# Where the look-ahead work of a chunked recurrent attention stands: one pair of heads ahead in two blocks, or up to two pairs ahead in pieces

## The chip, the cores and the metric

The kernel runs on one core of one Trainium2 chip. The metric is device time in microseconds, the median of repeated runs, and one further execution was recorded by the hardware profiler. Engines are named as in the profile: PE is TensorE's matmul, PEld its weight load, DVE is VectorE, ACT is ScalarE, POOL is GpSimd and SP is SyncE, which issues nearly all transfers here.

## What is computed

Two layers on x of shape 2 x 1024 x 512. Each layer adds to x the product of an attention part and a gated MLP of the layer-normalised input. The change touches the first layer's attention alone, a gated delta rule with 16 heads of 128:

```python
q = silu(causal_dwconv(x @ Wq, qcw, qcb))          # k and v in the same way
alpha = sigmoid(x @ Wa + ba); beta = sigmoid(x @ Wb + bb)
def step(S, inps):
    qt, kt, vt, at, bt = inps
    Sk = einsum('bhvk,bhk->bhv', S, kt)
    err = Sk - vt
    S = at * S - bt * (err[..., None] * kt[:, :, None, :])
    ot = einsum('bhvk,bhk->bhv', S, qt)
    return (S, ot)
o = layernorm(o) * ln_w + ln_b
return (o * sigmoid(x @ Wg)) @ Wo
```

Written step by step, this is 1024 dependent steps. The kernel computes it in chunks of 128 tokens. Inside a chunk the dependence is a lower triangular system, whose matrix L is built from k and the decays; the state S passes from one chunk to the next.

## The kernel before

Heads go in 8 pairs (index `hg`, 0 to 7). A pair holds two heads of two batches, so four sequences side by side, and has 8 chunks (`c`). Projections are made for two chunks at a time (`p`, 0 to 3).

For one pair the work has these parts. `project` (L448) makes q, k or v: matmuls at L455 into the two PSUM buffers `pa`, two evictions by ACT (L467, L471), three taps of the convolution on the DVE (L475), and SiLU on ACT (L483). The gate is projected in the pair's loop at L741. `ahead` (L486) makes for two chunks k, the decays e and the matrices L of 32 x 32 blocks (pkk at L506, lt at L508), and stores all three in DRAM. `invert` (L515) loads the diagonal blocks of all 8 chunks of a pair, 128 blocks on 128 partitions, and inverts them by 31 steps of a multiply into `tl` (L531) and a subtraction from `ml` (L538), each needing the one before, all on the DVE; then it stores them. Counting its set-up and its store, it hands out 33 steps. `within` (L548) loads e and the inverted blocks and makes what a chunk needs without the state. `across` (L586) is the chain of the recurrence: pks from the state (L599), rt on the DVE (L600), transposed into pr (L606), then four block steps of pw (L622), w4 by ACT (L624), pz (L616) and rr by the DVE (L621), then wt, the new state (L638, L644), the output po and its normalisation. `finish` (L678) transposes, gates and stores the previous chunk's output.

The stages in time are these. In the front the input is normalised and transposed and the first layer's MLP runs (48 steps in all, handed out by `some(n)`), with `ahead` and `invert` of pair 0 written between its steps. The front has one PSUM buffer each for `pa` and `pi`. The pairs follow. In pair `hg`, behind each of the chunks 0 to 3 stands a whole `ahead` of the next pair, one for each `p`; behind chunks 4 to 7 stand nine steps each of the next pair's inverse. So k, e, L and the inverse are all one pair ahead. After the last pair come the output projection, which is joined with the MLP's result, and then the second layer.

The order on each engine is not the written one. A scheduler places instructions at build time by modelled readiness, and the written order is the priority among those that are ready. On the chip each engine then works through its own list in that fixed order, with semaphores for the data. A list entry whose data are late holds up all that is behind it on its engine.

Of the kernel before, what the change touches and what calls it, by code (L numbers as in the profile page):

```python
# [19 lines left out]
DRAM = bass.MemoryType.DRAM  # L20
# [7 lines left out]
HG = H // 2  # L28
# [3 lines left out]
IC = INTER // P  # L32
# [20 lines left out]
def cols(ap, n):  # L53

    if len(ap.shape) == 2:
        ap = ap.unsqueeze(2)
    return ap.to_broadcast([ap.shape[0], ap.shape[1], n])


def rep(ap, n):  # L60

    return ap.unsqueeze(1).to_broadcast([ap.shape[0], n, ap.shape[1]])
# [150 lines left out]
def first_layer(ctx, tc, a, cst, minus_half, keep, xnT, od, gd, then):  # L213
# [23 lines left out]

    nc = tc.nc  # L240
    cp = keep

    early = ctx.enter_context(ExitStack())
    pa = early.enter_context(tc.tile_pool(name="at_a", bufs=2))
    kp = early.enter_context(tc.tile_pool(name="at_k", bufs=1))
    dr = ctx.enter_context(tc.tile_pool(name="at_d", bufs=2, space=DRAM))

    pools = {}

# [129 lines left out]
    def some(n):  # L379
        for _ in zip(range(n), beside):  # L380
            pass

    def load_weights(hg, names):
        w = {}
        for n in names:
            pool = kp if n == "wk" else pools["w"]
            w[n] = pool.tile([P, KC, 2 * P], F32, tag=n, name=f"{n}_{hg}")
            nc.sync.dma_start(
                w[n], a[n][:, hg * 256 : (hg + 1) * 256].rearrange("(kc p) n -> p kc n", p=P)
            )  # L390
        return w
# [56 lines left out]
    def project(j, n, hg, p, w, dst):  # L448

        u = f"{n}_{hg}_{p}"  # L450
        for hl in range(2):
            h = hg * 2 + hl
            pp = pools["a"].tile([P, B, 2 * P], F32, tag="pa", name=f"p{u}_{hl}")
            for kc in range(KC):
                nc.tensor.matmul(  # L455
                    pp,
                    lhsT=w[:, kc, hl * P : (hl + 1) * P],
                    rhs=xnT[:, kc, :, p * 2 * P : (p + 1) * 2 * P],
                    start=(kc == 0),
                    stop=(kc == KC - 1),  # L460
                )
            pre = pools["p"].tile([P, B, 2 * P + 4], F32, tag="pre", name=f"pre{u}_{hl}", bufs=3)
            if p == 0:
                nc.gpsimd.memset(pre[:, :, 0:3], 0.0)
            else:
                nc.gpsimd.tensor_copy(pre[:, :, 0:3], halo[:, j, hl, :, 0:3])
            nc.scalar.copy(pre[:, :, 3 : 2 * P + 3], pp)  # L467
            if p < NC // 2 - 1:
                nc.gpsimd.tensor_copy(halo[:, j, hl, :, 0:3], pre[:, :, 2 * P : 2 * P + 3])
            acc = dst[:, 2 * hl : 2 * hl + 2, :]  # L470
            nc.scalar.activation(  # L471
                acc, pp, AF.Identity, scale=cw[:, j, h, 3:4], bias=cb[:, j, h : h + 1]
            )
            for tap in range(3):
                nc.vector.scalar_tensor_tensor(  # L475
                    acc,
                    in0=pre[:, :, tap : tap + 2 * P],
                    scalar=cw[:, j, h, tap : tap + 1],
                    in1=acc,
                    op0=ALU.mult,  # L480
                    op1=ALU.add,
                )
        nc.scalar.activation(dst, dst, AF.Silu)  # L483


    def ahead(hg, p, w, store):  # L486
        u = f"{hg}_{p}"
        ka = pa.tile([P, NS, 2 * P], F32, tag="ka", name=f"ka_{u}")
        project(1, "wk", hg, p, w["wk"], ka)
        nc.sync.dma_start(store["k"][p], ka)  # L490
        for c in (2 * p, 2 * p + 1):
            col = c * H * B + hg * NS
            k = ka[:, :, (c % 2) * P : (c % 2 + 1) * P]

            e = pa.tile([P, NS, P + 4], F32, tag="e", name=f"e_{hg}_{c}", bufs=3)
            nc.gpsimd.memset(e[:, :, 0:1], 0.0)
            g_rows(hg, c, e[:, :, 1 : P + 1])
            nc.vector.tensor_tensor(e[:, :, 1 : P + 1], e[:, :, 1 : P + 1], rep(mask, NS), ALU.add)
            for s in range(NS):
                nc.scalar.activation(  # L500
                    e[:, s, 1 : P + 1], e[:, s, 1 : P + 1], AF.Exp, bias=bcol[:, col + s : col + s + 1]
                )
            nc.sync.dma_start(store["e"][c], e[:, :, 1 : P + 1])
            pkk = pools["i"].tile([P, NS, P], F32, tag="pi", name=f"pkk_{hg}_{c}")
            for s in range(NS):
                nc.tensor.matmul(pkk[:, s, :], lhsT=k[:, s, :], rhs=k[:, s, :], start=True, stop=True)  # L506
            lt = pa.tile([P, NS, P], F32, tag="lt", name=f"lt_{hg}_{c}")
            nc.vector.tensor_tensor(lt, pkk, e[:, :, 0:P], ALU.mult)  # L508
            for bl in range(4):
                nc.sync.dma_start(  # L510
                    store["l"][c, :, :, SLOT[bl] : SLOT[bl] + 4 - bl, :].rearrange("s i b t -> i s (b t)"),
                    lt[32 * bl : 32 * bl + 32, :, 32 * bl :],
                )

    def invert(hg, store):  # L515

# [172 lines left out]
    def new_store(hg):  # L689
        return {  # L690
            "k": dr.tile([NC // 2, P, NS, 2 * P], F32, tag="dk", name=f"dk_{hg}"),
            "e": dr.tile([NC, P, NS, P], F32, tag="de", name=f"de_{hg}"),
            "l": dr.tile([NC, NS, 32, 10, 32], F32, tag="dl", name=f"dl_{hg}"),
        }

    NP = NC // 2
    wk = load_weights(0, ("wk",))
    store = new_store(0)
    for p in range(NP):
        some(IC // 2)  # L700
        ahead(0, p, wk, store)
    for _ in invert(0, store):
        some(1)
    some(NTT * IC)
    front.close()
    for n, bufs in (("w", 2), ("g", 1), ("b", 2)):
# [9 lines left out]
    with tc.issue_after(last["act"].ins):  # L716
        late = None
        for hg in range(HG):
            w = load_weights(hg, ("wq", "wv", "wg"))
            state = None  # L720
            more = hg + 1 < HG
            if more:
                wk = load_weights(hg + 1, ("wk",))
                after = new_store(hg + 1)
                steps = invert(hg + 1, after)
            else:
                early.close()
                joining = then()
            for p in range(NP):
                u = f"{hg}_{p}"  # L730
                kb = pools["b"].tile([P, NS, 2 * P], F32, tag="kb", name=f"kb_{u}")
                nc.sync.dma_start(kb, store["k"][p])
                q = pools["b"].tile([P, NS, 2 * P], F32, tag="q", name=f"q_{u}")
                project(0, "wq", hg, p, w["wq"], q)
                v = pools["b"].tile([P, NS, 2 * P], F32, tag="v", name=f"v_{u}")
                project(2, "wv", hg, p, w["wv"], v)
                gate = pools["b"].tile([P, NS, 2 * P], F32, tag="gate", name=f"gate_{u}")
                for hl in range(2):
                    pg = pools["a"].tile([P, B, 2 * P], F32, tag="pa", name=f"pgate_{u}_{hl}")
                    for kc in range(KC):  # L740
                        nc.tensor.matmul(  # L741
                            pg,
                            lhsT=w["wg"][:, kc, hl * P : (hl + 1) * P],
                            rhs=xnT[:, kc, :, p * 2 * P : (p + 1) * 2 * P],
                            start=(kc == 0),
                            stop=(kc == KC - 1),
                        )
                    nc.scalar.activation(gate[:, 2 * hl : 2 * hl + 2, :], pg, AF.Sigmoid)
                for c in (2 * p, 2 * p + 1):
                    half = slice((c % 2) * P, (c % 2 + 1) * P)  # L750
                    parts = within(hg, c, q[:, :, half], kb[:, :, half], v[:, :, half], store)
                    state, on = across(hg, c, state, parts)
                    if late is not None:
                        finish(*late)
                        if not more and c in (1, 2):
                            joining.load_o()
                    late = (hg, c, gate[:, :, half], on)
                    if more:
                        if c < NP:
                            ahead(hg + 1, c, wk, after)  # L760
                        else:
                            for _ in zip(range(9), steps):
                                pass
            if more:
                for _ in steps:
                    pass
                store = after
        finish(*late)
    return joining

# [369 lines left out]
```

## Time and profile before

| | us |
|---|---|
| median of 3 runs (3357.73 to 3361.75) | 3358.22 |
| the profiled execution's own time | 3359.76 |
| its span | 3357.7 |
| front: start to the first projection of pair 0 | 0 to 324 |
| pairs 0 to 7: to the normalisation of the last chunk | 324 to 1860 |
| pair 1 (last chunk of pair 0 to last chunk of pair 1) | 195.1 |
| pair 6 | 189.5 |
| pair 7 | 150.4 |
| granted TensorE clock, mean | 0.998 |

The page of a profile begins with each engine's busy time as a share of the span, and then cuts the span into 40 slices of about 84 us, with the busy share of each in tenths. In this kernel the slices 5 to 22 are the pairs of heads. A row of the view of windows gives, for one stretch, its start and end, its length, and the busy time and count of each engine. A row of the view of waits gives who waited, for what, the sum, the number of times and the longest. In the timeline each row is a run of like instructions with its start, its duration and, in brackets, the idle time before it.

### The profile page before, as it was taken

How to read it: one execution, taken by the hardware profiler on the slowest of the kernel's cores; microseconds unless marked ns; L12 is line 12 of the kernel's file. 1: busy time of each engine (PE TensorE's matmuls, PEld its weight loads, DVE VectorE, ACT ScalarE, POOL GpSimd, SP SyncE). 2: the span in 40 equal slices, each digit the busy share in tenths (PEclk: the TensorE clock that was granted, in tenths of full speed). 3: DMA queues.
4: the chain of work that ended last, by engine and by line, in shares of the span. 5: the costliest groups of instructions: out<-in, count | busy, mean ns of one | idle time of the engine just before them, and what ended most of it. 6: DMA issues, size and time to landing. Idle time of an engine off the chain costs nothing.

```text
span 3357.7 us, 35998 instructions
## 1 busy us (share of the span) xinstructions
PE 3253.2 (97%) x11734; PEld 1803.9 (54%) x11734; DVE 2079.6 (62%) x4397; ACT 1425.9 (42%) x2480; POOL 865.9 (26%) x1520
## 2 busy tenths in 40 slices
PE   8999999999999999999999999999999999999998
PEld 6677565656565665656566444444444444444443
DVE  4445676676867677686855623666666655555545
ACT  3453676767677677767666000222222200110002
POOL 2000334343343435344344200111121100000102
PEclk9999999999999999999999999999999999999999
DMA  5122443434434343433351653111111100000003
GB/s 168 56 73 77 119 122 102 109 86 126 109 87 127 101 108 87 125 105 95 91 141 43 194 153 101 35 32 32 31 32 32 44 25 19 19 23 22 19 0 125
DMA packets 428699, 268.21 MB, mean 80 GB/s; under 512 B 193888, under 2 KB 368480, under 8 KB 428512
## 3 DMA queue, kind: packets, MB, share of 16 engines
q1 hardware_dynamic: 418208, 248.87, 26.2%
q0 software_dynamic: 5696, 8.65, 0.9%
q10 hardware_dynamic: 4608, 8.39, 0.7%
q8 instruction: 94, 1.54, 0.2%
q14 instruction: 93, 0.76, 0.1%
HBM read 179.71 MB, written 86.11 MB: 79 GB/s over the span
## 4 chain that ended last, share of the span: by engine, by line
PE 43%; DVE 6%; ACT 2%; issue 2%; POOL 2%; DMA 0%; POOLq 0%; DVEq 0%; ACTq 0%
PE po L1005 10%; PE jpo L183 6%; PE pgc L928 3%; PE pgd L928 3%; PE puc L928 3%; PE pua L928 3%; PE pga L928 3%; PE pud L928 3%; PE pgb L928 1%; PE pub L928 1%; DVE ga L886 1%; PE pgate L741 1%; PE pwk L455 1%; PE pwv L455 1%; PE pr L871 1%
## 5 line engine op out<-in xcount | busy, mean ns | idle before, releaser
L1005 PE MATMUL po<-w_d,u 128*128 128x512 f32 x1024 | 456.8, 599 | 10.9 <-DVE acc L1016 5.4
L1005 PEld LDWEIGHTS po<-w_d,u 128*128 128x128 f32 x1024 | 190.0, 190 | 272.0 <-issue 207.3
L948 ACT COPY g<-pga 128x512 f32<-128x512 f32 x32 | 18.7, 586 | 640.1 <-PE pga L928 640.1
L629 POOL COPY wt<-w 32x128 f32<-32x128 f32 x512 | 233.2, 456 | 113.4 <-ACT w L624 91.8
L455 PE MATMUL pwq<-xnT,wq 128*128 128x512 f32 x512 | 251.3, 593 | 0.0
L455 PE MATMUL pwv<-xnT,wv 128*128 128x512 f32 x512 | 240.3, 599 | 9.1 <-ACT q L471 8.4
L455 PE MATMUL pwk<-xnT,wk 128*128 128x512 f32 x512 | 247.0, 594 | 0.0
L1016 DVE TENSOR_TENSOR acc<-acc,po 128x512 f32<-128x512 f32 x240 | 163.0, 682 | 135.6 <-PE po L1005 134.5
L741 PE MATMUL pgate<-xnT,wg 128*128 128x512 f32 x512 | 238.8, 593 | 0.1
L183 PE MATMUL jpo<-wo,jo 128*128 128x512 f32 x512 | 225.0, 592 | 0.0
L475 DVE SCALAR_TENSOR_TENSOR ka<-prewk,cw,ka 128x512 f32<-128x512 f32 x192 | 151.2, 788 | 65.4 <-ACT ka L471 54.8
L475 DVE SCALAR_TENSOR_TENSOR q<-prewq,cw,q 128x512 f32<-128x512 f32 x192 | 149.8, 780 | 55.9 <-ACT q L471 53.8
L475 DVE SCALAR_TENSOR_TENSOR v<-prewv,cw,v 128x512 f32<-128x512 f32 x192 | 155.7, 827 | 42.8 <-ACT v L471 40.6
L622 PEld LDWEIGHTS pw<-rr,ground 128*128 128x128 f32 x512 | 88.8, 188 | 169.8 <-DVE rr L621 121.3
L974 ACT ACTIVATE g<-g 128x512 f32<-128x512 f32 x96 | 60.4, 630 | 261.1 <-DVE g L938 260.9
L616 PEld LDWEIGHTS pz<-w,ground 128*128 128x128 f32 x768 | 119.7, 190 | 84.3 <-ACT w L624 51.2
L183 PEld LDWEIGHTS jpo<-wo,jo 128*128 128x128 f32 x512 | 95.0, 191 | 107.1 <-issue 107.1
L616 PE MATMUL pz<-w,ground 128*128 128x128 f32 x768 | 140.7, 283 | 8.0 <-ACT w L624 8.0
L455 PEld LDWEIGHTS pwv<-xnT,wv 128*128 128x128 f32 x512 | 91.3, 191 | 104.9 <-issue 83.4
L832 POOL TENSOR_TENSOR w_g<-w_g 128x256 f32<-128x256 f32 x16 | 11.9, 741 | 503.8 <-DVE w_g L818 503.8
L673 ACT ACTIVATE on<-po,nm,rs 128x128 f32<-128x128 f32 x256 | 96.3, 457 | 107.0 <-DVE nm L668 107.0
L622 PE MATMUL pw<-rr,ground 128*128 128x128 f32 x512 | 107.4, 292 | 31.2 <-DVE rr L621 27.9
(246 smaller groups left out, 6806.6 us busy)
## 6 DMA issues: line engine op xcount, KB each, us to landing
e<-gr SPq DMA_DIRECT2D x64, 256.0 KB, 4.4
de<-e SPq DMA_DIRECT2D x64, 256.0 KB, 2.6
dk<-ka SPq DMA_DIRECT2D x32, 512.0 KB, 2.8
kb<-dk SPq DMA_DIRECT2D x32, 512.0 KB, 4.7
eb<-de SPq DMA_DIRECT2D x64, 256.0 KB, 2.8
eg<-gr SPq DMA_DIRECT2D x64, 256.0 KB, 3.8
od<-ot SPq DMA_DIRECT2D x64, 256.0 KB, 2.1
jo<-od SPq DMA_DIRECT2D x16, 1024.0 KB, 6.4
```

The lines of the kernel that those rows point to most:

```text
L183: nc.tensor.matmul(po, lhsT=ot[:, h, :], rhs=self.wo[h], start=(h == 0), stop=(h == H - 1))
L455: nc.tensor.matmul(pp, lhsT=w[:, kc, hl * P : (hl + 1) * P], rhs=xnT[:, kc, :, p * 2 * P : (p + 1) * 2 * P], start=(kc == 0), stop=(kc == ...
L475: nc.vector.scalar_tensor_tensor(acc, in0=pre[:, :, tap : tap + 2 * P], scalar=cw[:, j, h, tap : tap + 1], in1=acc, op0=ALU.mult, op1=ALU.add,
L616: nc.tensor.matmul(pz[:, bl, :], lhsT=G[:, SLOT[bb] + bl - bb, :], rhs=w4[:, bb, :], start=(bb == 0), stop=(bb == bl - 1),)
L622: nc.tensor.matmul(pw[:, bl, :], lhsT=G[:, SLOT[bl], :], rhs=rr[:, bl, :], start=True, stop=True)
L629: nc.gpsimd.tensor_copy(dst, w4[r, bl])
L673: nc.scalar.activation(on[:, s, :], po[:, s, :], AF.Identity, scale=rs[:, s : s + 1], bias=nm[:, s : s + 1])
L741: nc.tensor.matmul(pg, lhsT=w["wg"][:, kc, hl * P : (hl + 1) * P], rhs=xnT[:, kc, :, p * 2 * P : (p + 1) * 2 * P], start=(kc == 0), stop=( ...
L928: nc.tensor.matmul(banks[key], lhsT=w[:, i, par, :], rhs=q[:, j, par, :], start=(first and par == 0), stop=(par == 1), skip_group_check=no ...
L974: nc.scalar.activation(ge[key], x, AF.Gelu_apprx_tanh)
L1005: nc.tensor.matmul(po, lhsT=inter[par, h][:, i * P : (i + 1) * P], rhs=wd[:, par, :], start=(par == 0), stop=(par == 1),)
L1016: nc.vector.tensor_tensor(dst, dst, po, ALU.add)
```

## The change

It does four things.

- Where the work made ahead stands. k, e and L are now made two pairs ahead, and the inverse one pair ahead. Pair `hg` therefore has beside it `ahead` of pair `hg + 2` and `invert` of pair `hg + 1`. `ahead` of pairs 0 and 1 and the inverse of pair 0 are in the front; the inverse of pair 1 stands in pair 0. Pair 6 has only an inverse beside it, pair 7 nothing.
- How it is cut. `project` hands over after each of its two heads, and `ahead` after each chunk, so one `ahead` has four pieces and a pair's four have 16. Behind every chunk stand four steps of the inverse (five behind chunk 0) and two pieces.
- The priority of `across` is raised by 40 places.
- The DRAM pool has three buffers rather than two, since three pairs' k, e and L are alive at once. In the front, three MLP steps rather than five stand ahead of each `ahead` of pair 0, and each `ahead` of pair 1 stands behind one step in six of the inverse of pair 0.

```diff
+def done(steps):
+    for _ in steps:
+        pass
...
-    dr = ctx.enter_context(tc.tile_pool(name="at_d", bufs=2, space=DRAM))
+    dr = ctx.enter_context(tc.tile_pool(name="at_d", bufs=3, space=DRAM))
...
                     op0=ALU.mult,
                     op1=ALU.add,
                 )
+            yield
         nc.scalar.activation(dst, dst, AF.Silu)
...
-        project(1, "wk", hg, p, w["wk"], ka)
+        yield from project(1, "wk", hg, p, w["wk"], ka)
...
                     lt[32 * bl : 32 * bl + 32, :, 32 * bl :],
                 )
+            yield
...
+    stores = [new_store(0), new_store(1)]
     wk = load_weights(0, ("wk",))
-    store = new_store(0)
     for p in range(NP):
-        some(IC // 2)
-        ahead(0, p, wk, store)
-    for _ in invert(0, store):
+        some(3)
+        done(ahead(0, p, wk, stores[0]))
+    wk = load_weights(1, ("wk",))
+    for i, _ in enumerate(invert(0, stores[0])):
         some(1)
+        if i % 6 == 1 and i // 6 < NP:
+            done(ahead(1, i // 6, wk, stores[1]))
     some(NTT * IC)
...
             w = load_weights(hg, ("wq", "wv", "wg"))
             state = None
+            store = stores[hg]
             more = hg + 1 < HG
             if more:
-                wk = load_weights(hg + 1, ("wk",))
-                after = new_store(hg + 1)
-                steps = invert(hg + 1, after)
+                steps = invert(hg + 1, stores[hg + 1])
             else:
                 early.close()
                 joining = then()
+            if hg + 2 < HG:
+                wk = load_weights(hg + 2, ("wk",))
+                stores.append(new_store(hg + 2))
+                aheads = itertools.chain.from_iterable(
+                    ahead(hg + 2, p, wk, stores[hg + 2]) for p in range(NP)
+                )
...
-                project(0, "wq", hg, p, w["wq"], q)
+                done(project(0, "wq", hg, p, w["wq"], q))
...
-                    state, on = across(hg, c, state, parts)
+                    with tc.high_priority(40):
+                        state, on = across(hg, c, state, parts)
...
                     if more:
-                        if c < NP:
-                            ahead(hg + 1, c, wk, after)
-                        else:
-                            for _ in zip(range(9), steps):
-                                pass
-            if more:
-                for _ in steps:
-                    pass
-                store = after
+                        done(itertools.islice(steps, 4 if c else 5))
+                    if hg + 2 < HG:
+                        done(itertools.islice(aheads, 2))
```

More of the change, by code (lines that the diff above doesn't have):

```diff
@@ L733, in first_layer @@
                 q = pools["b"].tile([P, NS, 2 * P], F32, tag="q", name=f"q_{u}")
-                project(0, "wq", hg, p, w["wq"], q)
+                done(project(0, "wq", hg, p, w["wq"], q))
                 v = pools["b"].tile([P, NS, 2 * P], F32, tag="v", name=f"v_{u}")
-                project(2, "wv", hg, p, w["wv"], v)
+                done(project(2, "wv", hg, p, w["wv"], v))
                 gate = pools["b"].tile([P, NS, 2 * P], F32, tag="gate", name=f"gate_{u}")
```

## The prediction, made before the changed kernel was run

> **What bounds the kernel now.** I read the page first: busy shares, then the slices.
>
> ```profile
> PE 3253.2 (97%) x11734; PEld 1803.9 (54%) x11734; DVE 2079.6 (62%) x4397; ACT 1425.9 (42%) x2480; POOL 865.9 (26%) x1520
> ...
> PE   8999999999999999999999999999999999999998
> ...
> DVE  4445676676867677686855623666666655555545
> ```
>
> TensorE is in use almost throughout, so the kernel is a stream of matmuls, and what a reordering can win is the time in which that stream stands still. The busy share hides part of it, because the recorded ends of matmuls overlap. I therefore take the pitch from the timeline: six 128x512 matmuls of pwq took 2.74 us with a last one of 0.59, so (2.74 - 0.59) / 5 = 0.43 us each; eight 128x128 ones took 1.06 with a last one of 0.28, so 0.111 us each. What a stretch lasts beyond count times pitch is lost. Next I read stretches bounded by the 4th and 8th chunk of a pair of heads (where nm is written): pair 1 in two halves, then the first half of the last pair, which has nothing made ahead beside it.
>
> ```profile
> 546.60:640.60 94.00, 92.32 (x449) 59.68 (x447) 60.83 (x141) 65.17 (x126) 38.44 (x80) 1.00 0.38 111
> 640.60:741.70 101.10, 93.88 (x427) 57.10 (x426) 79.01 (x195) 71.90 (x125) 42.98 (x76) 1.00 0.40 101
> ...
> 1709.10:1788.90 79.80, 77.58 (x401) 51.73 (x400) 46.64 (x120) 47.63 (x92) 33.85 (x64) 1.00 0.38 101
> ```
>
> The columns are length, then PE, PEld, DVE, ACT, POOL busy with counts. Filtered to the projection lines L455 and L741, the wide matmuls are 110 + 16, 83 + 48 and 64 + 32. First half: 126 x 0.43 + 323 x 0.111 = 90.1, so 3.9 us lost of 94.0. Second: 131 x 0.43 + 296 x 0.111 = 89.2, so 11.9 lost of 101.1. Last pair: 96 x 0.43 + 305 x 0.111 = 75.1, so 4.7 lost. The second half differs from both others in one thing, the inverse: filtered to tile tl, its 62 VectorE operations take 27.54 us between 660 and 714, where the DVE is busy 50.73 of 54 us. So the inverse, packed as it is, costs about 11.9 - 3.9 = 8 us per pair, and all else about 3.9 per half. The timeline inside that stretch shows how:
>
> ```profile
> 705.85 0.38 PE L616 MATMUL pz<-w,ground 128*128 128x128 f32 x2
> ...
> 706.44 0.34 DVE L531 TENSOR_TENSOR tl<-ll,ml 128x175 f32<-128x175 f32 x1
> ...
> 706.81 0.34 DVE L538 TENSOR_TENSOR ml<-ml,tl 128x175 f32<-128x175 f32 x1
> ...
> 707.19 0.32 DVE L531 TENSOR_TENSOR tl<-ll,ml 128x156 f32<-128x156 f32 x1
> 707.55 0.32 DVE L538 TENSOR_TENSOR ml<-ml,tl 128x156 f32<-128x156 f32 x1
> 707.90 0.30 DVE L531 TENSOR_TENSOR tl<-ll,ml 128x135 f32<-128x135 f32 x1
> 708.12 0.28 DVE L621 TENSOR_TENSOR rr<-rr,pz 128x128 f32<-128x128 f32 x1
> ...
> 708.46 0.49 PE L622 MATMUL pw<-rr,ground 128*128 128x128 f32 x2 [1.36 <-DVE rr L621]
> ```
>
> pz is done near 706.3, but five operations of the inverse stand before rr in the DVE's queue; pw waits for rr, and PE stands 1.36 us although projections are queued behind it. Over the span this wait is the largest of the recurrence:
>
> ```profile
> PEld pw L622 <- DVE rr L621: 121.3, 188, 2.2
> ...
> DVE rr L621 <- PE pz L616: 100.2, 68, 3.8
> ```
>
> **What the Trainium skill says.** "Perfetto Trace Analysis", section "Identifying the Most-Contended Engine", says that matmul busy time does not tell how near TensorE is to its limit; the trace agrees, 92.32 us busy in a stretch that needs 90.1. Its section "Optimization Strategy" says that kernels whose busiest engine changes may gain by interleaving the regimes: that is what the change attempts, and here the DVE goes from 60.83 busy us in one half to 79.01 in the other. "TensorE: Matmul & The Clock Gate", section "Architectural detail", says that the DVE's queue is strictly first in, first out; the five operations before rr agree. "SBUF — State Buffer", section "SBUF: two separate sides", says that a DVE operation with two SBUF inputs and a GpSimd one exclude each other; the trace agrees, ml of 128x207 took 1.15 us beside a GpSimd multiply, and its neighbours of similar size 0.36.
>
> **The change part by part.**
>
> 1. Moves, no work added. One `ahead` is 64 wide matmuls and 64 narrow ones (pkk, 512 over 8 pairs): 64 x 0.43 + 64 x 0.111 = 34.6 us of PE. `ahead` of pair 1 goes from pair 0 into the front beside the MLP, and so on down: pairs 0 to 5 still have one each, pair 6 has none now. The front is PE-bound too (from 230 to 324 us PE is busy 92.95 of 94), so it grows by 34.6 and pair 6 shrinks by 34.6: 0 net.
>
> 2. The even share. Behind each chunk now come two pieces of `ahead` and four steps of the inverse, instead of a whole `ahead` (first four chunks) or nine steps (last four). In pairs 0 to 5 the floor is 2 x 3.9 = 7.8 us lost. Of the 8 us for the inverse, between nothing (perfectly spread) and all 8 (packed elsewhere) remain. The front speaks against perfect spreading: there each inverse step is written beside one MLP step of about 5.4 us (24 matmuls at 0.227), yet all 62 operations ran within 32 us (21.14 busy between 265 and 297). The DVE's order evidently follows readiness, not the written place. The inverse of the next pair is now ready from the start of a pair, so some packing stays. I take the middle, 4: a pair loses 11.8 in place of 15.8, 6 x -4 = -24 us.
>
> 3. Pair 6 has an inverse but no k work: floor as in the last pair, 2 x 4.7, plus 4 = 13.4. Before, 189.5 us for 252 wide and 606 narrow matmuls = 175.7, lost 13.8. Change -0.4. Pair 7: 0.
>
> 4. The front gets four more `ahead`s, with one PSUM buffer each for pa and pi and ACT evictions between; MLP matmuls cover them. Lost 0 to 8, taken 3. In return the inverse of pair 1 may finish there: 0 to -8 for pair 0, taken 0.
>
> 5. `across` 40 places ahead in priority: it goes before `within` of its chunk, on which it partly depends, and before the last pieces made ahead. What it can win is the waits of pr on rt (7.0 + 6.7 us, weight load and matmul) and of pks on state (4.3 + 2.9), so about -10. What it can lose: a chain operation placed at the earliest moment stands at the head of PE's queue with projections behind it. The last pair, where nothing older is left, loses 4.7 per four chunks, not 3.9: 0.2 per chunk x 64 = +13. Taken 0.
>
> 6. Queues. The DMAs of `ahead` (k, e in and out, eight pieces of L per two chunks) are the same number on SP, each a pair earlier, so every load of them has more slack; landing is 2.6 to 4.7 us. wk has one buffer: its load now follows the last projection of the previous pair's `ahead`, and the first use is behind the next chunk 0, over 20 us later against 6.2 us to land. GpSimd's memset of ml waits for the store of the previous inverse (3.0 us to land), with halo copies behind it: 0 to +3 per pair, taken 0, since the store was issued before. The third DRAM buffer costs nothing.
>
> Sum: -24 - 0.4 + 3 = -21.4 on the profiled 3359.8 us (span 3357.7 and 2.1 around it): 3338; the median is 1.5 lower, so 3337.
>
> **Rivals.**
> - The packed inverse only moves (like the front). For: the 32 us run there. Against: in pairs it competes with more DVE work, which thins it. Six pairs 0, pair 6 +3.6 (9.4 + 8 - 13.8), front +3, inverse of pair 1 out of pair 0, -8: -1.4, so 3357.
> - Slower: the inverse falls on k's DVE work. In 660 to 714 the other DVE work is 23.2 of 54 us, 43%; k's (24 taps of 0.79 and 16 operations of 0.68 on e and lt, 30 of a pair's 195 us) adds 15%. At 94% busy the inverse gets 36%, so it lasts 27.5 / 0.36 = 76 us rather than 54. The packed stretch lost 11.9 - 47 x 0.041 = 10 us in 54, 0.184 per us, against 0.041 elsewhere: 76 x 0.184 + 119 x 0.041 = 18.9, +3.1 per pair, x 6 = +19, pair 6 +3.6, front +3: 3384. It decides once a pair has more than about 60 us with the DVE above 90%. For: the same head-of-queue wait at rr. Against: lower density per chunk may be absorbed by the 1 us of projections between chain steps.
>
> **How the numbers follow.** Spread as in step 2: 0.53. Only moved: 0.20. Slower: 0.27. A measurement tells 0.2%, 6.7 us, from no change. The first is nearly all faster (0.51 of 0.53), the second gives 0.03 to faster and 0.13 to same and 0.04 to slower: faster 0.54, same 0.15, slower 0.31. Low end: the inverse's 8 us gone in six pairs (-48) and some of step 5, 3304. High end: most of the way to the slower case, 3372. The likeliest case alone is 3304 to 3352.
>
> **What would show it.** Right: stretches of 25 us in pairs 1 to 5 with the DVE between 65% and 85% throughout, each pair about 191 us, pair 6 near 154, the front 35 to 38 us longer, pw waiting on rr well under 121 us. Wrong: a stretch of 50 us or more with the DVE above 90% early in each pair; pairs of 195 us or more; a growing wait on rr, or GpSimd waiting on ml's store.

## The result, and the profile after

The changed kernel takes 3386.54 us (median of 6 runs, 3385.94 to 3390.0) where the kernel before, run beside it, takes 3358.72 (3356.65 to 3361.75). The ratio is 1.0083, 95% interval 1.007 to 1.0096: slower by 28 us, and outside the predicted range. The profiled execution has a span of 3384.0 us against 3357.7. First the page of the changed kernel: busy shares, the slices of VectorE, and one group of the matmuls.

```profile
PE 3268.6 (97%) x11734; PEld 1808.2 (53%) x11734; DVE 2110.1 (62%) x4397; ACT 1435.2 (42%) x2489; POOL 852.3 (25%) x1520
...
DVE  4564766768777676867555633666666655555545
...
L758 PE MATMUL pgate<-xnT,wg 128*128 128x512 f32 x512 | 238.1, 615 | 24.6 <-ACT v L477 24.2
```

The matmuls are the same 11734 and the shares are the same to a point, TensorE's slices are the same digit for digit, so little on this page but the last line says where 26 us went: the gate's projection, which hardly waited before (0.1 us), now waits 24 us for ScalarE to empty v's PSUM bank. What tells more is the count the prediction used, length less 0.43 us for each wide matmul and 0.11 for each narrow one. These are pairs 2 and 3 of the changed kernel by their windows (length, then PE, PEld, DVE, ACT and POOL busy with counts, granted clock, DMA share, GB/s).

```profile
766.70:965.20 198.50, 190.01 (x873) 118.29 (x872) 146.39 (x335) 136.74 (x250) 81.63 (x156) 0.98 0.39 104
965.20:1162.70 197.50, 187.27 (x873) 117.07 (x872) 145.90 (x335) 136.66 (x250) 81.97 (x156) 1.00 0.38 104
```

Pairs 1 to 5 need 177.8 us in both kernels (256 wide, 616 narrow), so a length of 198.5 is 20.7 us lost. Done for every stage (in the front with 0.227 us for the MLP's matmuls, as in the prediction):

| stage | length before | after | lost before | lost after |
|---|---|---|---|---|
| front | 324.2 | 360.1 | 26.5 | 27.8 |
| pair 0 | 222.4 | 210.6 | 20.9 | 24.1 |
| pairs 1 to 5, mean | 194.6 | 197.1 | 16.7 | 19.2 |
| pair 6 | 189.4 | 168.7 | 14.9 | 20.3 |
| pair 7 | 150.5 | 157.4 | 10.8 | 16.3 |
| the rest | 1498.2 | 1501.8 | 35.2 | 33.7 |

The lost time grows by 3.2 us in pair 0, 12.5 in the five pairs together, 5.4 and 5.5 in the last two, 1.3 in the front and -1.5 in the rest: 26.4, where the spans differ by 26.3. The two agree by construction, because both kernels have the same matmuls; what the count tells is in which stage the time is lost. (Lengths of pairs 0, 6 and 7 also shift because some matmuls fall on the other side of a boundary; the lost column is free of that.)

The waits inside the pairs come next: before, then after, as instruction, what it waited for, us in total, times, longest.

```profile
PE pw L622 <- DVE rr L621: 27.9, 38, 1.4
...
PE pz L616 <- ACT w L624: 8.0, 9, 1.7
PE pr L606 <- DVE rt L600: 6.7, 8, 1.1
```

```profile
PE pgate L758 <- ACT v L477: 24.2, 21, 2.8
PE pz L625 <- ACT w L633: 19.1, 39, 1.2
PE pr L615 <- DVE rt L609: 14.9, 23, 1.5
PE pw L631 <- DVE rr L630: 5.3, 15, 1.0
```

The wait that the prediction wanted gone is nearly gone, 27.9 to 5.3 us. Three others grew: +24 at the gate, +11 at pz, +8 at pr. All waits of PE in the pairs together rise from 62.7 to 71.9 us, so they account for 9 of the 27 us more that the pairs lose; matmuls at half clock, below, are another part. And the inverse is not spread. The quarters of pair 2 in the changed kernel, bounded by every second chunk: the first with all engines, then all four with tile tl alone, where the columns are length, DVE busy with count, clock, DMA share, GB/s.

```profile
766.70:822.10 55.40, 54.23 (x235) 32.61 (x234) 48.91 (x116) 38.94 (x75) 22.98 (x43) 1.00 0.42 107
```

```profile
766.70:822.10 55.40, 16.57 (x42) 1.00 0.42 107
822.10:869.70 47.60, 6.77 (x20) 0.93 0.26 65
869.70:918.60 48.90, 0.00 (x0) 1.00 0.37 102
918.60:965.20 46.60, 0.00 (x0) 1.00 0.50 142
```

Written as four steps behind each of eight chunks, its 62 operations run in the first half of the pair, 42 and 20 by quarters, and none later. In the kernel before the same quarters had 0, 0, 41 and 21: it is as packed as it was, only at the other end. The DVE is at 48.91 / 55.40 = 88% there.

The timeline at the end of that first quarter shows one of the new waits (start, length, engine, line, operation, and in brackets the idle time before it with what ended it).

```profile
820.02 2.74 PE L758 MATMUL pgate<-xnT,wg 128*128 128x512 f32 x6
...
820.62 1.44 POOL L675 TENSOR_TENSOR rs<-rs,minus_half 128x4 f32<-128x4 f32 x1 [2.44 <-ACT eg L570]
...
822.04 1.26 POOL L572 TENSOR_TENSOR kg<-kb,eg 128x512 f32<-128x512 f32 x1
822.10 1.22 DVE L677 SCALAR_TENSOR_TENSOR nm<-mv,rs 128x4 f32<-128x4 f32 x1 [0.90 <-POOL rs L675]
...
823.35 1.51 ACT L682 ACTIVATE on<-po,nm,rs 128x128 f32<-128x128 f32 x4 [2.26 <-DVE nm L677]
...
824.74 0.79 ACT L477 ACTIVATE v<-pwv,cb,cw 128x512 f32<-128x512 f32 x1
...
825.58 2.07 PE L758 MATMUL pgate<-xnT,wg 128*128 128x512 f32 x2 [2.82 <-ACT v L477]
```

ScalarE stands at `on`, which waits 2.26 us for nm, which waits for GpSimd's rs. nm itself takes 1.22 us here, beside GpSimd's multiply kg of 1.26 us; its shortest take 0.16 us. Over 0.9 us it takes in 30 of the 64 chunks, in the kernel before in 13. Behind `on` in ScalarE's queue is the eviction of v, and TensorE stands 2.82 us until that is done. The windows from there on show TensorE's clock.

```profile
825.50:832.50 7.00, 6.92 (x11) 3.07 (x12) 6.55 (x21) 5.64 (x7) 0.19 (x1) 0.55 0.00 1
832.50:840.00 7.50, 7.50 (x35) 4.58 (x34) 2.82 (x6) 4.85 (x8) 1.80 (x6) 1.00 0.47 89
```

For 7 us after the stall the granted clock is 0.55, and 11 matmuls run where 35 run in the next 7.5 us.

### The profile page after: what moved, and what is told of

Its sections match the earlier page's. It is cut to its first block, busy times and chain, and to the rows that moved or that the text cites. A ratio compares the mean times of both kernels' runs of the same rounds, so it can differ in the third digit from the quotient of the medians.

```text
span 3384.0 us, 35976 instructions
## 1 busy us (share of the span) xinstructions
PE 3268.6 (97%) x11734; PEld 1808.2 (53%) x11734; DVE 2110.1 (62%) x4397; ACT 1435.2 (42%) x2489; POOL 852.3 (25%) x1520
## 4 chain that ended last, share of the span: by engine, by line
PE 40%; DVE 6%; ACT 3%; issue 2%; POOL 1%; DMA 0%; POOLq 0%; ACTq 0%; SPq 0%; DVEq 0%
PE po L1017 10%; PE jpo L188 6%; PE pgc L940 3%; PE pgd L940 3%; PE puc L940 3%; PE pua L940 3%; PE pga L940 3%; PE pud L940 3%; PE pgb L940 1%; PE pub L940 1%; DVE ga L898 1%; PE pr L883 1%; PE pwq L461 1%; PE pz L625 1%; DVE u L992 0%
## 5 line engine op out<-in xcount | busy, mean ns | idle before, releaser
L1017 PEld LDWEIGHTS po<-w_d,u 128*128 128x128 f32 x1024 | 189.4, 190 | 270.8 <-issue 206.1
L638 POOL COPY wt<-w 32x128 f32<-32x128 f32 x512 | 218.0, 426 | 184.6 <-ACT w L633 161.7
L758 PE MATMUL pgate<-xnT,wg 128*128 128x512 f32 x512 | 238.1, 615 | 24.6 <-ACT v L477 24.2
L481 DVE SCALAR_TENSOR_TENSOR v<-prewv,cw,v 128x512 f32<-128x512 f32 x192 | 164.8, 868 | 38.5 <-ACT v L477 33.5
L481 DVE SCALAR_TENSOR_TENSOR ka<-prewk,cw,ka 128x512 f32<-128x512 f32 x192 | 165.9, 864 | 30.1 <-ACT ka L477 27.3
L481 DVE SCALAR_TENSOR_TENSOR q<-prewq,cw,q 128x512 f32<-128x512 f32 x192 | 157.8, 822 | 32.8 <-ACT q L477 30.5
L758 PEld LDWEIGHTS pgate<-xnT,wg 128*128 128x128 f32 x512 | 96.3, 195 | 139.1 <-issue 101.5
L625 PE MATMUL pz<-w,ground 128*128 128x128 f32 x768 | 145.5, 289 | 19.3 <-ACT w L633 19.1
L631 PEld LDWEIGHTS pw<-rr,ground 128*128 128x128 f32 x512 | 89.2, 188 | 121.6 <-DVE rr L630 76.5
L630 DVE TENSOR_TENSOR rr<-rr,pz 128x128 f32<-128x128 f32 x192 | 54.4, 283 | 149.7 <-PE pz L625 149.3
L844 POOL TENSOR_TENSOR w_g<-w_g 128x256 f32<-128x256 f32 x16 | 11.8, 739 | 492.9 <-DVE w_g L830 492.9
```

The lines of the kernel that those rows point to most:

```text
L481: nc.vector.scalar_tensor_tensor(acc, in0=pre[:, :, tap : tap + 2 * P], scalar=cw[:, j, h, tap : tap + 1], in1=acc, op0=ALU.mult, op1=ALU.add,
L625: nc.tensor.matmul(pz[:, bl, :], lhsT=G[:, SLOT[bb] + bl - bb, :], rhs=w4[:, bb, :], start=(bb == 0), stop=(bb == bl - 1),)
L631: nc.tensor.matmul(pw[:, bl, :], lhsT=G[:, SLOT[bl], :], rhs=rr[:, bl, :], start=True, stop=True)
L638: nc.gpsimd.tensor_copy(dst, w4[r, bl])
L758: nc.tensor.matmul(pg, lhsT=w["wg"][:, kc, hl * P : (hl + 1) * P], rhs=xnT[:, kc, :, p * 2 * P : (p + 1) * 2 * P], start=(kc == 0), stop=( ...
L1017: nc.tensor.matmul(po, lhsT=inter[par, h][:, i * P : (i + 1) * P], rhs=wd[:, par, :], start=(par == 0), stop=(par == 1),)
```

## The experiments

All are run beside the kernel before on the same chip (3359.85 to 3361.66 us in these runs); a ratio is to that, with its 95% interval. "Lost" is the count above, as a mean of pairs 1 to 5, where the kernel before has 16.7 and the changed one 19.2. It is read from one profiled execution of each kernel. Six results fell outside every range that was stated ahead of them: no_inverse, after_no_inverse, k_blocks, moved_only, priority_only and spread_priority.

### What the inverse costs

The kernel before without the 62 VectorE operations of each inverse (the elimination is left out, the rest of `invert` stays), and later the same cut in the changed kernel.

```diff
-            nc.vector.tensor_tensor(
-                tv,
...
-            rest = m[:, 0, i + 1 :, : i + 1]
-            nc.vector.tensor_tensor(rest, rest, tv, ALU.subtract)
```

> The kernel before without the 62 VectorE operations of each inverse (left out of the computation; loads, the unit matrix and stores stay). The prediction's price, 8 us per pair in seven pairs: faster by about 56 us, 3303. If the stretches lose time for another reason than the inverse: faster by less than 20.

> The changed kernel without the 62 VectorE operations of each inverse (left out of the computation). Theory I: over 40 us faster than the changed kernel, under 3347. Theory F: as in the kernel before, some 20 to 25 us faster, 3362 to 3367.

no_inverse: 3338.46 us, 0.9932 [0.9917, 0.9947]; lost 12.9. All the VectorE work of seven inverses in the pairs and one in the front is worth 22 us, 3.8 per pair in pairs 1 to 5, not the 8 of the prediction. The windows of the halves of its pair 3 show why the subtraction was wrong.

```profile
928.10:1020.10 92.00, 91.83 (x445) 59.28 (x445) 60.40 (x140) 64.49 (x122) 35.69 (x79) 1.00 0.39 113
1020.10:1118.70 98.60, 92.53 (x430) 57.64 (x429) 56.45 (x133) 74.08 (x129) 41.98 (x78) 1.00 0.40 104
```

With no inverse at all, and with the DVE at 57% of the second half, that half still loses 8.8 us (98.6 less 84 + 48 wide and 298 narrow matmuls at the prediction's pitches) against 2.4 in the first (92.0, with 110 + 16 and 319). The two halves hold nearly the same matmuls (132 wide and 298 narrow, 126 and 319); ScalarE is busy 74.08 us in the second and 64.49 in the first, but that this is the reason wasn't tested. The prediction had put the whole difference down to the inverse.

after_no_inverse: 3376.06, 1.0047 [1.0032, 1.0062]; lost 19.5. Its pairs 2 and 6:

```profile
764.30:961.80 197.50, 187.80 (x874) 116.72 (x873) 128.18 (x274) 137.34 (x251) 78.52 (x156) 1.00 0.39 105
1553.50:1715.30 161.80, 155.84 (x758) 100.65 (x757) 92.81 (x237) 99.82 (x190) 69.90 (x136) 1.00 0.35 97
```

Without any inverse on the DVE the new arrangement is still 16 us slower than the kernel before with its inverses, and 38 us slower than no_inverse, which has none either. So all that is not the inverse costs 38 us, and the inverse, 22 us in the kernel before, costs 10 to 12 here. None of that lies in pairs 1 to 5, which lose 19.5 without it and 19.2 with it; about 5.5 lie in pair 0 and 7 in pair 6, which is 161.8 us long here and 168.7 with the inverse. The burst of the DVE early in a pair isn't what makes the change slow.

### Where the inverse runs, and how k's work is cut

Without the raised priority, the two halves of the even share one at a time. no_priority keeps both:

```diff
-                    with tc.high_priority(40):
-                        state, on = across(hg, c, state, parts)
+                    state, on = across(hg, c, state, parts)
```

and the others change one or two lines on top of that.

```diff
 # k_blocks: whole aheads behind the first four chunks
-                        done(itertools.islice(aheads, 2))
+                        done(itertools.islice(aheads, 4 if c < NP else 0))
 # k_spread_whole: whole aheads behind every second chunk
-                        done(itertools.islice(aheads, 2))
+                        done(itertools.islice(aheads, 0 if c % 2 else 4))
 # inverse_late: k in even pieces, the inverse behind the last four chunks
-                        done(itertools.islice(steps, 4 if c else 5))
+                        done(itertools.islice(steps, 9 if c >= NP else 0))
 # moved_only: the lines of k_blocks and of inverse_late together
```

> The changed kernel without the raised priority of across, all else as changed. Theory P (the raised priority costs: the normalisation of across is put ahead of the evictions of PSUM on ACT, so that pgate waits for v, and the chain stands at the head of PE's queue): 3345 to 3365 us, and the last pair back near 150.5 us from 157.4. Theory K (the placement of the pieces and of the inverse costs): 3380 us or more, pairs 1 to 5 still lose 17 to 21 us each.

> The changed kernel without the raised priority, and with a whole ahead (four pieces) behind each of chunks 0 to 3 as before, two pairs ahead; the inverse stays at four steps behind every chunk. Theory F (k's projections, cut to an even share, no longer fill PE while it waits for the chain; as whole blocks they do): 3345 to 3368, some 40 us less than the 3404.6 of the same kernel with even pieces. Theory I (the inverse, now ready at a pair's start, holds up its first chunks): 3385 or more.

> The changed kernel without the raised priority, with the inverse's nine steps behind each of chunks 4 to 7 as before, and k, decays and L in even pieces two pairs ahead. Theory I: 3345 to 3368. Theory F: 3385 or more.

> The changed kernel without the raised priority and with both at their old places behind the chunks (whole aheads at 0 to 3, nine steps at 4 to 7): what is left of the change is that k, decays and L are two pairs ahead, and the front. Theories F and I alike: within 10 us of before, 3350 to 3370. If the move by a pair costs in itself (front, loads, the missing k work in pair 6): 3375 or more.

> As k_blocks (no raised priority, inverse written at four steps a chunk), but the four whole aheads stand behind chunks 0, 2, 4 and 6 and not behind 0 to 3: evenly spread, not cut. If spreading k's work is what costs (chunks with half the filling lose more than a full and an empty one together): 3395 to 3410, as with even pieces (3404.6). If the cutting into pieces costs: 3375 to 3385, as k_blocks (3380.4).

| kernel | k's work | inverse written | us | ratio | lost |
|---|---|---|---|---|---|
| moved_only | whole, first half | late | 3374.81 | 1.0044 [1.0029, 1.0059] | 16.8 |
| k_spread_whole | whole, every second chunk | even | 3377.79 | 1.0051 [1.0036, 1.0066] | 17.4 |
| k_blocks | whole, first half | even | 3380.36 | 1.0061 [1.0045, 1.0078] | 17.2 |
| no_priority | even pieces | even | 3404.64 | 1.0133 [1.0116, 1.0149] | 22.9 |
| inverse_late | even pieces | late | 3435.87 | 1.0228 [1.0211, 1.0245] | 27.8 |

Three things follow. First, being two pairs ahead already costs about 15 us with everything else as before (moved_only): 2 in the front and 12 in pairs 0, 6 and 7, nothing in pairs 1 to 5. Second, whole aheads or pieces is the large step: k_spread_whole and no_priority differ in that alone, and the pieces cost 44 - 16 = 28 us, nearly all of it in pairs 1 to 5 (5.5 each). Third, the place where the inverse is written doesn't decide where it runs. Tile tl in the two halves of pair 3, for k_blocks and then inverse_late:

```profile
981.50:1077.50 96.00, 0.00 (x0) 1.00 0.41 115
1077.50:1179.30 101.80, 26.69 (x62) 1.00 0.36 94
```

```profile
992.50:1100.00 107.50, 22.58 (x62) 0.97 0.31 83
1100.00:1196.70 96.70, 0.00 (x0) 1.00 0.45 121
```

Written even (k_blocks) it runs late, written late (inverse_late) it runs early. In each it runs soon after the pieces of L that it needs have been stored: in k_blocks the last of them is issued at 1080 us and the first step of the inverse runs at 1098, in inverse_late at 977 and 1011. With whole aheads early in a pair L is ready in the middle of it; with aheads stretched over the pair L is ready at its end, and the inverse runs at the start of the next one.

The written place isn't free, though. On whole aheads it makes 5.5 us (k_blocks against moved_only), but on pieces inverse_late is 31 us slower than no_priority, although in both the inverse runs in the first half of the pair. The gate's wait for v is 37.2 us in inverse_late and 21.1 in no_priority, pz's for w 15.3 and 5.2. Why that is so is not shown.

What the pieces change shows in the waits of TensorE in the pairs: no_priority, then k_spread_whole.

```profile
PE pw L631 <- ACT rr L617: 27.0, 25, 1.9
PE pr L615 <- DVE rt L609: 22.4, 18, 3.7
PE pgate L758 <- ACT v L477: 21.1, 19, 2.0
```

```profile
PE pw L631 <- ACT rr L617: 22.7, 26, 2.1
PE pw L631 <- DVE rr L630: 20.2, 32, 4.5
PE pr L615 <- DVE rt L609: 17.6, 7, 3.2
PE pgate L758 <- ACT v L477: 9.3, 13, 2.8
```

The gate's wait for v's eviction is 12 us longer, pr's for rt 5 and pw's for ScalarE's rr 4; the wait on VectorE's rr is 14 shorter (6.4 in no_priority). These four rise by 7 us in sum, all of PE's waits in the pairs by 11 (76.2 to 87.5). The stalls also leave more half clock behind: added up over the pairs from the clock record, 47.6 us at half speed in no_priority, 17.0 in k_spread_whole, 17.0 in the changed kernel and 3.4 in the kernel before. Matmuls at half speed lose half of such a stretch, so this can be up to 15 of the 28 us, and with the waits up to 26; at the net price found at the end of this document (1 us for 6.8 us at half speed) it would be about 5. Half clock isn't needed for a loss, though: after_no_inverse has no half clock in the pairs and loses 19.5 per pair.

One guess was that a piece that ends before k's SiLU puts that activation in a bad place on ScalarE. cut_after_silu moves the SiLU into the piece before it, on top of no_priority.

```diff
-            yield
+            if hl == 0:
+                yield
         nc.scalar.activation(dst, dst, AF.Silu)
+        yield
```

> The changed kernel without the raised priority, with ahead cut into four pieces as there, but k's SiLU is in the second piece with the second head's projection, and no longer left over until behind the next chunk. If the SiLU left behind the next chunk (and with it pkk and L) is what the cut costs: 3375 to 3388. If any cut costs: 3395 to 3410, as with the cut before the SiLU (3404.6).

3403.47 us, 1.0124 [1.0109, 1.0139], lost 22.1: no difference beyond the intervals. The guess fell.

### An inverse that is really spread

Here the order is tied: the multiply of each step is kept in program order, so that it can't run far from where it is written.

```diff
-            nc.vector.tensor_tensor(
+            first = nc.vector.tensor_tensor(
...
+            if hg:
+                tc.keep_in_program_order(first)
```

> The kernel before, with the multiply of every inverse step tied behind all that was written earlier for the DVE, so that the nine steps behind chunks 4 to 7 run there and not in one stretch as soon as L is ready. If the packing in one stretch is what an inverse costs (22 us in all by no_inverse): 3340 to 3352. If the number of its operations between the chain's matters, wherever they are: 3355 to 3365. If the inverse comes too late for the next pair: 3375 or more.

> The changed kernel with its inverse steps tied to their written places in the same way: four behind each chunk, so that the even share, which the changed kernel's trace does not show, is made real. If the packed stretch at a pair's start is what costs: 3360 to 3372 (after_no_inverse, 3376, bounds it, so a larger gain than 10 us would be a surprise). If k's even pieces cost: 3376 or more.

> k_blocks (whole aheads behind chunks 0 to 3, two pairs ahead) with the inverse's steps tied to four behind each chunk. In k_blocks the inverse runs half a pair before its written place, beside chunks 4 to 7. If an inverse spread over eight chunks costs less than one in a stretch: 3360 to 3372, and the waits of pw for rr fall below those of k_blocks. If not: 3378 or more.

> k_blocks_pinned (3383.2), with the last inverse (for pair 7) free to run when its L is ready. If pair 7's loss of 36 us came from the late inverse: 3360 to 3366, and no long stretch at half clock near 1750 us. If not: 3378 or more.

before_pinned (tie alone, in the kernel before) 3438.38, 1.023 [1.0215, 1.0246]: the inverse for pair 2 ends at 761 us, behind the last chunk of pair 1 (759), where it had ended 28 us ahead of that. That this lateness is the cause was expected, and not tested further. after_pinned 3413.49, 1.0157 [1.0141, 1.0174]: in the changed kernel a really spread inverse (30 and 32 operations in the halves of pair 3) is 27 us slower than the packed one, lost 21.7. k_blocks_pinned (with k_blocks' lines) 3383.2, 1.0066 [1.0051, 1.0081]. In that one the inverse is truly even; tile tl in the halves of pair 3:

```profile
968.00:1065.60 97.60, 9.12 (x30) 1.00 0.43 109
1065.60:1163.20 97.60, 16.42 (x32) 0.98 0.35 102
```

Its pairs 1 to 5 lose 15.5 on average against 17.2 in k_blocks and 16.7 before: an even inverse is worth 1.2 to 1.7 us per pair by this run and about 1 by the next, where the prediction took 4. These are small beside the spread of single pairs, 12.6 to 19.3 in the two runs. Its pair 7 lost 36.0, since the tied inverse of the last pair ended too late:

```profile
1746.06 0.77 PE L633 MATMUL pw<-rr,ground 128*128 128x128 f32 x2 [7.28 <-DMA ground<-dl]
```

pinned_but_last leaves the last pair's untied (`if 0 < hg < HG - 1`): 3364.75, 1.0016 [1.0009, 1.0023]. Lost 15.8, and pair 7 back to 12.8. It is the nearest to the kernel before that this arrangement came, and doesn't beat it. In its profiled execution pairs 0 to 5 win 6 us of lost time, pair 6 loses 12 more than before (26.9), the front 3 and pair 7 2.

### The raised priority

```diff
 # priority_only: in the kernel before
-                    state, on = across(hg, c, state, parts)
+                    with tc.high_priority(40):
+                        state, on = across(hg, c, state, parts)
```

```diff
 # priority_chain: inside across, with the block around its call taken away
+        with tc.high_priority(40):
+            rt = pools["b"].tile([P, 4, NS, 32], F32, tag="rt", name=f"rt_{u}")
...
-                    with tc.high_priority(40):
-                        state, on = across(hg, c, state, parts)
+                    state, on = across(hg, c, state, parts)
```

priority_chain is the changed kernel with the raised block only around the recurrence, from rt to the new state, the output's product and its normalisation at the ordinary place. spread_priority, blocks_tied_priority and spread_tied_priority are k_spread_whole, pinned_but_last, and pinned_but_last with k_spread_whole's line, each with the raised priority.

> The kernel before with nothing but the raised priority of across by 40. Theory P: slower by 15 to 35 us, 3373 to 3393. Theory K: within 7 us of before.

> The changed kernel with the priority raised for the recurrence alone (from rt to the new state), and no longer for po, its statistics and the normalised output. If it is the output's normalisation on ACT that holds up the evictions: 3345 to 3368 us and pgate's wait for v (24 us on PE) gone. If it is the chain itself that stands too early in PE's queue: 3375 to 3390.

> k_spread_whole (3377.8) with the priority of across raised by 40. If the priority mends only what the cut lost: no gain, 3373 to 3400. If it is worth 18 us in itself: 3355 to 3363.

> pinned_but_last (3364.8: whole aheads behind chunks 0 to 3, inverse tied to four steps behind each chunk but for the last pair's) with the priority of across raised. If the three gains add: 3350 to 3358, faster than before. If priority and tied steps hold each other up on the DVE (the tied steps wait for the end of across): 3365 or more.

> The same with the whole aheads behind chunks 0, 2, 4 and 6 (spread_priority was 3369.7). If the gains add: 3350 to 3358. If not: 3365 or more.

| kernel | without priority | with it | ratio with it |
|---|---|---|---|
| kernel before (priority_only) | 3360.8 | 3398.16 | 1.0114 [1.0099, 1.0129] |
| k_spread_whole (spread_priority) | 3377.79 | 3369.65 | 1.0026 [1.0017, 1.0034] |
| no_priority (the changed kernel) | 3404.64 | 3386.54 | 1.0083 [1.007, 1.0096] |
| no_priority (priority_chain) | 3404.64 | 3387.83 | 1.0084 [1.0069, 1.0099] |
| pinned_but_last (blocks_tied_priority) | 3364.75 | 3428.68 | 1.0205 [1.0191, 1.0219] |
| spread and tied (spread_tied_priority) | not run | 3413.85 | 1.016 [1.0146, 1.0174] |

The same edit is +37, -8, -18 and +64 us, by what it is put on. priority_chain gives the time of the changed kernel, so that `on` was raised with the rest isn't what makes the changed kernel slow, although v's eviction stands behind it at 824 us. The gate's wait for v is 12.7 us there in place of 24.2, but pr's wait for rt is 40.6 in place of 14.9. The waits of priority_only in the pairs:

```profile
PE pw L622 <- DVE rr L621: 19.1, 14, 1.8
PE pgate L741 <- ACT v L471: 14.1, 6, 3.0
...
PE pk L576 <- DVE at L581: 12.3, 6, 4.2
```

pw's wait on rr falls from 27.9 to 19.1, but the waits of the gate, which isn't in this view of the kernel before, and of pk (3.8 before) grow, and so does pr's (12.4 in place of 6.7). That work of `within` and evictions of projections now stand behind the recurrence would explain it, and is not shown.

### Is 28 us more than a reshuffle?

Any edit changes the schedule everywhere, so one edit that should do nothing: in the kernel before, the front's MLP steps ahead of each `ahead` as in the change.

```diff
-        some(IC // 2)
+        some(3)
```

> The kernel before with three MLP steps in place of five ahead of each ahead of pair 0, and nothing else: no work is added or moved between pairs. What it differs by is what a reshuffled schedule does by itself: within 5 us of before if the schedule is robust, more if single stalls come and go with it.

3363.18 us, 1.0009 [1.0002, 1.0016]. Pairs 1 to 5 lose 16.8 against 16.7. The mean of these pairs repeats to 0.1 us although what is ahead of them moved (single pairs by up to 1), so differences of 2.5 and 5.5 per pair are well above what this one reshuffle does. Its edit is in the front; a reshuffle inside the pairs was not tried. It also shows that in the kernel before this detail of the change is worth some 3 us.

## Why the prediction was wrong

The predicted 3337 us is 50 below the result. By its steps:

- **Reading the bound: right.** TensorE's stream is the limit: it is busy 97% in both kernels, and count times pitch leaves 16.7 of 194.6 us lost in a pair before and 19.2 of 197.1 after.
- **Step 1, moves: right for the moved work.** The front grew by 35.9 us, 34.6 of it moved work. That nothing else follows from being two pairs ahead was wrong: moved_only costs 15, of which pairs 0, 6 and 7 have 12. Why pair 0 loses 5 and pair 7 loses 6 more in it wasn't tested.
- **Step 2, the even share: the step that failed.** It let pairs 0 to 5 lose 11.8 us each, a floor of 2 x 3.9 = 7.8 for all else and 4 for the inverse; pairs 1 to 5 of the changed kernel lose 19.2. The term that failed is the floor: without any inverse a pair loses 12.9 in the kernel before and 19.5 in the new arrangement. It was too low from the start, because "the inverse, packed as it is, costs about 11.9 - 3.9 = 8 us per pair" is 3.8 measured: the half that this was read from loses 8.8 without any inverse, so the halves differ in more than the one thing named. And the change raised it, which the step put at nothing without a reason: cutting `ahead` into pieces costs 5.5 us per pair (before the priority takes some of it back), and was counted as free. The share itself was a lesser error. The inverse, which the step itself suspected of following readiness, wasn't spread at all (62 operations in the first half of a pair), yet taking it out of the changed kernel wins nothing in these pairs. A really spread one won 1 to 1.7 us per pair on whole blocks and made the changed kernel slower. The -24 would have needed nearly the whole measured price of six inverses, 6 x 3.8 = 23.
- **Step 3, pair 6.** Predicted 13.4 us lost, measured 20.3. The floor of 9.4 was too low here too: without the inverse this pair loses about 13.4, and the inverse adds 7 where 4 was taken. Pair 7, taken as unchanged, lost 16.3 in place of 10.8.
- **Step 4, the front: right.** +3 taken, +1.3 measured.
- **Step 5, the priority: wrong, and outside its bounds on both sides.** It was taken as 0 within -10 and +13. It is -17 on the pieces, so the change would have been slower without it, and +37 in the kernel before. The wait it hoped to shorten, pr on rt, fell on the pieces (22.4 to 14.9, no_priority against the changed kernel) and grew in the kernel before (6.7 to 12.4), and the loss named as a risk was sized from a single comparison, the last pair's 4.7 us against 3.9.
- **Step 6, queues: not seen to matter** in the changed kernel; GpSimd waits once for ml's store (10.1 us; 56.0 in the kernel before), and PE 0.8 us for a load of wk.
- **What would show it.** pw's wait on rr fell from 121.3 to 76.5 us (weight loads, whole span), which had been named as a sign of success. It fell, and the pairs grew: a wait that shrinks is a sign only if none grows beside it. Of the signs of failure, pairs of 195 us or more came, and a stretch of 55 us with the DVE at 88%, just short of the 90% named; "a growing wait on rr" did not.
- **The slower rival gave 3384 us**, near the measured 3386.5, but not by its mechanism. It needed about 60 us above 90% on the DVE and a longer wait on rr, and neither came; it put +19 on the inverse in six pairs, where in pairs 1 to 5 the changed kernel loses as much without its inverse (19.5) as with it. The match is a coincidence.

The path from the kernel before to the changed one is then, from the ratios: +17 for two pairs ahead with whole aheads spread over the pair (k_spread_whole), +28 for cutting these into pieces (no_priority), -17 for the priority (-18 by the medians alone). The terms depend on the order: on whole aheads the priority wins 8, alone it loses 37.

What stays open: which instruction of a piece does the harm. The waits name ScalarE's evictions (v, rr, w) and rt, the SiLU's place in its piece is excluded, and up to half of it may be half clock after the stalls; no run separates these further. Open too is why a written place of the inverse that hardly moves it costs 31 us on pieces.

## What to carry to other kernels

Price an operation by taking it out on the chip, or from two stretches that differ in nothing else: two halves of one loop lost 2.4 and 8.8 us here with the operation taken out of both. Where a scheduler places instructions by readiness, writing work evenly doesn't spread it; look at where the trace has it, and expect it soon after its last input is there. When a wait falls, look at once for the waits that grew: here the one on rr fell by 23 us, waits for ScalarE's evictions of PSUM grew by more, and whole blocks of filler did better than small even pieces.

## What the runs showed of the hardware

A short stall of TensorE can be followed by matmuls at half clock. In the 7 us from 825.5 us on, behind the stall of 2.82 us, the granted clock was 0.55; in no_priority a stall of 2.88 us at pr was followed by 7.2 us at 0.59. Not each one brings it: pairs 2, 3 and 4 of the changed kernel have the same stall at the same place (2.82, 2.82 and 2.83 us), and pair 3 keeps a clock of 1.00. The traces show what differs. All stretches at half clock in the pairs of a run begin on one grid of 3.413 us; in the changed kernel they begin at 381.2, 825.0 and 1220.9 us, 130 and 116 steps apart. On this grid, with length, PE busy with its count, granted clock, DMA share and GB/s, the two steps about the stall are, in pair 2 and then in pair 3:

```profile
821.62:825.03 3.41, 1.14 (x3) 0.99 0.03 9
825.03:828.45 3.42, 2.87 (x4) 0.50 0.01 2
```

```profile
1019.56:1022.97 3.41, 1.67 (x4) 1.00 0.20 58
1022.97:1026.38 3.41, 2.33 (x6) 1.00 0.00 0
1026.38:1029.80 3.42, 3.42 (x18) 1.00 0.00 0
1029.80:1033.21 3.41, 1.92 (x9) 1.00 0.00 0
```

In pair 2 most of the stall falls into one step, 2.3 us of it idle, and the next two steps run at half clock; in pair 3 it is cut by a border, 1.7 and 1.1 us. Counted in this way over the pairs in the traces of all runs, each of the 99 steps with more than 2.01 us idle was followed by half clock, while steps idle from 1.7 to 2.0 us went either way.

"TensorE: Matmul & The Clock Gate" of the Trainium skill, section "What's actually happening", gives the idle clock as half of full speed, granted after an idle window of about 3.4 us that runs free of the kernel. The half speed and the grid agree with the trace; a window that is idle throughout was not needed here.

Pair 3 is only 1.0 us shorter than pairs 2 and 4 (197.5 against 198.5). So the net price of such a stretch was about 1 us there, though 7 us at half speed would suggest 3.5. Part of what the slow matmuls lose is taken from waits that would have come after: in the step from 1029.80 us pair 3 idles 1.5 us, where pair 2 at the same place is busy throughout (3.41 of 3.41 us from 831.86).
